# First 1x1 layer of a ConvNeXt block in fifteen products for eighteen, and the next image's first layernorm moved into fc1

## The chip, the core and the metric

The kernel runs on one core of a Trainium2 chip. The metric is the device time of one execution in microseconds (us). One execution was also recorded by the hardware profiler; the profile's stretches and timelines are counted from the start of that execution's span.

## What is computed

Eight images of 384 channels and 32 x 32 pixels go through two layers, all in fp32. Layer 0 is a transformer block, layer 1 a ConvNeXt block:

```python
# layer 0, on tokens (1024 per image, 384 wide), 8 heads of 48
xn  = layernorm(x);  q, k, v = xn @ w_qkv.T + b_qkv
x1  = softmax(q @ k.T * SCALE) @ v @ w_proj.T + b_proj + x
y   = x1 + gelu(layernorm(x1) @ w_fc1.T + b_fc1) @ w_fc2.T + b_fc2      # 384 -> 1536 -> 384
# layer 1
c   = depthwise_conv7x7(y) + dw_b
h   = gelu(layernorm(c) @ w1 + b1)                                      # 384 -> 1536
gx  = sqrt(sum over pixels of h**2);  nx = gx / (mean(gx) + eps)
out = y + (gamma * (h * nx) + beta + h) @ w2 + b2                       # 1536 -> 384
```

## The kernel before

Activations lie with channels on the 128 partitions and the 1024 pixels in the free dimension: three tiles of 128 channels (CT), twelve of the hidden width (HT), two halves of 512 pixels. A matrix product writes one PSUM bank of 128 x 512. TensorE (PE) does each such fp32 product in two passes, so the profile counts two matmuls for one in the source.

**Stages.** The loop over images interleaves two of them: after image b has gone through qk, attention, fc1 and fc2, the 1x1 layers w1 and w2 of image b-1 follow, with the values (v) of image b+1 between them. TensorE's order in the middle of the run is thus: qk(b), attention(b), fc1(b), fc2(b), w1(b-1), v(b+1), w2(b-1), qk(b+1). The last image is done apart, in pieces. VectorE (DVE) does the depthwise convolution of image b from w2(b-1) on, across the next image's attention; ScalarE (ACT) and accumulating DMAs from GpSimd (POOL) help it with seven taps per channel tile (`help_convolution`).

**Order of work.** The order is written out: nothing is rescheduled[...]. The class `Flow` keeps side work next to TensorE's: `flow.pe(us)` counts TensorE's time, and a chain (a generator) that yields a wait is continued when the count has come that far. `flow.finish(chain)` issues what is left of it. `after(first, chain)` starts a chain when another has ended.

**Fewer products.** fc2, w2 and qk multiply 3 x 3 by 3 x 2 blocks with fifteen products for eighteen. In fc2 and w2 (`by_thirds`) the hidden width is cut in three thirds of four tiles; the combinations of activations e, f, g, h, d are made in place between the fifteen products (four pairs of passes each, so 60 products), by DVE and, for `adding(g, f)`, `adding(h, b32)` and `adding(g, b32)`, by accumulating DMAs of 512 KB from POOL (`hid<-hid`, `y<-y`). In qk (`tiles_by_thirds`) one product is a single 128 x 512 one; its ten combinations of the input are made ahead by ten DVE subtractions and additions, `thirds_of`. The combined weights (`FORMS`) are made once, while image 0 is in attention, and kept in DRAM.

w1 (`grn_up`) works on six pairs of tiles; each takes eleven products for twelve, on four differences of the input that `block_differences` puts into `attn`. A `Weights` ring of nine tiles loads from SyncE's (SP) queue in the order of a plan; `used` frees a tile and issues the next load.

**Layernorms.** Per image there are three: ln1 before qk and the values, ln2 before fc1, ln3 before w1. `abreast` runs both halves of one side by side. Channel sums are made by folding the 128 partitions to 64 with an accumulating DMA from POOL (`ln_a<-ln_a`, `ln_sq<-ln_sq`, `attn<-attn`), then multiplying by ones on TensorE: two half-array products for each of sum and variance of each half. DVE adds, subtracts the mean and scales; ACT squares and takes rstd as exp(-0.5 ln(var + eps)).

Where ln1 and ln3 stand is decided by `conv_norm` (called in fc1, when ln2's second half is spawned) and `next_norms` (called at the end of fc1):

```python
        def conv_norm(b, ln):
            ...
                state["norm3"] = flow.spawn(after(ln, after(state["help"], after(state["conv"], norm))))
        def next_norms(b):
            ...
                state["norm1"] = flow.spawn(after(state["norm3"], norm, 50 if b else 11))
        def next_values(b):
                flow.finish(state["norm1"])
                state["thirds"] = flow.spawn(qk_thirds(b, state["xn"]))
                values(b, state["xn"])
```

So ln3 of image b-1 runs at the start of fc2(b), and ln1 of image b+1 in w1(b-1); for image 0, ln1 of image 1 runs in fc2(0). The tile `xn` has one buffer: it holds the normalized input of ln1, then that of ln2.

Of the kernel before, what the change touches and what calls it, by code (L numbers as in the profile page):

```python
# [51 lines left out]
P = 128  # L52
# [123 lines left out]
def block_kernel(  # L176
# [10 lines left out]
    w1: bass.AP,  # L187
    w2: bass.AP,
# [20 lines left out]
    s_w1 = dram.tile([P, HT // 2, 4, P], F32, tag="s_w1", bufs=1, name="s_w1")  # L209
# [7 lines left out]
    def load_x(b, tag, parts=2, engine=nc.sync):  # L217
        xt = one.tile([P, CT, N], F32, tag=tag, name=f"{tag}_{b}")
        src = image_of(x, b).rearrange("(c p) n -> p c n", p=P)
        for i in range(parts):  # L220
            cols = slice(i * N // parts, (i + 1) * N // parts)
            engine.dma_start(out=xt[:, :, cols], in_=src[:, :, cols])
        return xt

    vec = const.tile([P, NVEC], F32, name="vec")
    wqkv = const.tile([P, 3 * CT * C], F32, name="wqkv")
    wqk_sb = wqkv[:, : 2 * CT * C].rearrange("p (c m o) -> p c m o", c=CT, o=P)
    wv_sb = wqkv[:, 2 * CT * C :].rearrange("p (c o) -> p c o", c=CT)
    wproj_sb = const.tile([P, CT, C], F32, name="wproj_sb")
    ident = const.tile([P, P], F32, name="ident")  # L230
# [9 lines left out]
    third_e = const.tile([P, NH], F32, name="third_e")  # L240
# [112 lines left out]
    def plan_w1(tag, fast=True):  # L353
        plan = []
        for i in range(NC):
            plan.append(((f"w1_{tag}", i, "A"), chunk(w1, i)))
            if fast:
                plan.append(((f"w1_{tag}", i, "S"), s_w1[:, i, :, :].rearrange("p j o -> p (j o)")))
        return plan
# [28 lines left out]
    def thirds_of(src, places, e):  # L388

        b11, b12, b21, b22, b31, b32 = (src[:, s, half(n)] for s in range(CT) for n in range(2))  # L390
        f, h, e2, g, f2, h2, g2, f3, d = places
# [12 lines left out]
        return steps, (b12, b21, e, b22, f, h, e2, g, b31, f2, h2, g2, f3, b32, d)  # L404

# [138 lines left out]
    def weight_places(name):  # L544

        tiles = [three.tile([P, 2, NH], F32, tag="p", name=f"{name}_{i}") for i in range(2)]
        return [t[:, j, :] for t in tiles for j in range(2)]

# [30 lines left out]

    def qk(b, xn, weights=None):  # L580
# [3 lines left out]
        big = one.tile([P, HT * N], F32, tag="big", name=f"qk_{b}")  # L584
        parts = big[:, : 2 * NP * N].rearrange("p (i m n) -> p i m n", i=2, m=NP)
        if b == 0:
            spare_sums.append(big[:, 2 * NP * N :])
# [148 lines left out]
    def attention(b, xt, qT, kT, last_tile, ready, first):  # L736
# [44 lines left out]
        for n in range(len(steps) + 2):  # L781
# [10 lines left out]
            if n - 2 == len(steps) // 2 + 6:  # L792
                for chain in first:
                    flow.finish(chain)
                xn = one.tile([P, CT, N], F32, tag="xn", name=f"xn2_{b}")
# [20 lines left out]
    def exact_attention(xt, qT, kT):  # L816

        nc.vector.memset(attn, 0.0)
        for qt in range(N // P):
# [295 lines left out]
    def block_differences(acc):  # L1115

        b11, b12, b21, b22 = (acc[:, s, half(n)] for s in range(2) for n in range(2))
        t1, t2, t3, t4 = (attn[:, i, :] for i in range(4))
        yield 3.0
        for dst, one_, other in ((t1, b12, b11), (t2, b22, t1), (t3, b22, b12), (t4, b21, t2)):  # L1120
            nc.vector.tensor_tensor(dst, one_, other, ALU.subtract)
            yield 1.2

    def grn_up(b, acc, weights, tag):
# [5 lines left out]
        b11, b12, b21, b22, b31, b32 = (acc[:, s, half(n)] for s in range(CT) for n in range(2))  # L1130
        t1, t2, t3, t4 = (attn[:, i, :] for i in range(4))
        wa = f"w1_{tag}"
        spent = {}

        def finish(m):
            other_table(y[:, m, :], y[:, m, :], AF.Gelu, bias=b1[:, m : m + 1])

        def squares(i):
            for m in (i, i + HT // 2):
                waste = spent[i].rearrange("p a n -> p (a n)")  # L1140
                nc.scalar.activation(waste, y[:, m, :], AF.Square, accum_out=gx[:, m : m + 1])

        for i in range(HT // 2):
            j = i + HT // 2
            raw, sums = weights.at(wa, i, "A"), weights.at(wa, i, "S")
            a11, a12, a13, a22, a23 = (raw[:, k, :] for k in range(5))
            s1, s2, s3, s4 = (sums[:, k, :] for k in range(4))
            spent[i] = ps_s.tile([P, 2, NH], F32, tag="s", name=f"h_{b}_{i}_5")
            p5 = spent[i][:, 0, :]
            c11, c12, c21, c22 = (y[:, m, half(n)] for m in (i, j) for n in range(2))  # L1150

            def product(*pairs):
                bank = o_tile(f"h_{b}_{i}")
                accumulate(bank, list(pairs))
                return bank

            def plus(dst, bank, part):
                nc.vector.tensor_tensor(dst, bank, part, ALU.add)  # L1158

            nc.scalar.copy(c21, product((a11, b11)))  # L1160
            if i:
                finish(j - 1)
                squares(i - 1)
            plus(c11, product((a13, b31), (a12, b21)), c21)
            accumulate(p5, [(s1, t1)])
            plus(c21, product((s2, t2)), c21)
            plus(c12, p5, c21)
            plus(c12, product((s4, b22), (a13, b32)), c12)
            finish(i)
            plus(c21, product((s3, t3)), c21)  # L1170
            plus(c22, p5, c21)
            plus(c21, product((a23, b31), (a22, t4)), c21)
# [791 lines left out]
```

## Time and profile before

| | |
|---|---|
| time, median of 3 runs | 3287.62 us (3286.76 to 3288.6) |
| profiled execution: its time, its span | 3286.43 us, 3284.5 us |
| mean granted TensorE clock | 0.996 |
| busy: PE, DVE, ACT, POOL | 3262.0, 2413.3, 1630.0, 481.8 us |
| products `h` (w1), 792 passes in images 0 to 5 | 66 products an image |
| DVE additions of w1, `y<-h,y` | 288, 198.1 us, mean 690 ns |

A stage's length is read from the start of its first matmul to the start of the next stage's first. Ends of matmuls are modelled and overlap the next one, so a stage's lost time is its length less its passes, not less its busy time. In a timeline a line has the start, the duration, the engine, the source line, the operation, what it writes and reads, and in brackets how long the engine had been idle and what ended that.

### The profile page before, as it was taken

How to read it: one execution, taken by the hardware profiler on the slowest of the kernel's cores; microseconds unless marked ns; L12 is line 12 of the kernel's file. 1: busy time of each engine (PE TensorE's matmuls, PEld its weight loads, DVE VectorE, ACT ScalarE, POOL GpSimd, SP SyncE). 2: the span in 40 equal slices, each digit the busy share in tenths (PEclk: the TensorE clock that was granted, in tenths of full speed). 3: DMA queues.
4: the chain of work that ended last, by engine and by line, in shares of the span. 5: the costliest groups of instructions: out<-in, count | busy, mean ns of one | idle time of the engine just before them, and what ended most of it. 6: DMA issues, size and time to landing. Idle time of an engine off the chain costs nothing. (4 is left out here: it accounts for less than half of the span.)

```text
span 3284.5 us, 38862 instructions
## 1 busy us (share of the span) xinstructions
PE 3262.0 (99%) x14288; PEld 1410.0 (43%) x14288; DVE 2413.3 (73%) x3220; ACT 1630.0 (50%) x2243; POOL 481.8 (15%) x567
## 2 busy tenths in 40 slices
PE   9999999999999999999999999999999999999999
PEld 5334444443344434444334443444434444444455
DVE  4444787787867878678786787867887788879850
ACT  3542763447634375353762646526474365723631
POOL 2111210112110121101211012110221112200000
PEclk9999999999999999999999999999999999999999
DMA  6336733647345563536536374273843637433231
GB/s 236 115 109 146 166 61 78 154 111 171 60 97 144 135 139 58 127 116 169 102 61 140 106 188 82 56 169 87 202 74 61 179 88 189 74 79 85 68 91 54
DMA packets 202160, 380.08 MB, mean 116 GB/s; under 512 B 41072, under 2 KB 47088, under 8 KB 201328
## 3 DMA queue, kind: packets, MB, share of 16 engines
q0 software_dynamic: 80928, 161.78, 26.7%
q1 hardware_dynamic: 120752, 215.09, 21.3%
q8 instruction: 114, 1.87, 0.2%
q10 hardware_dynamic: 288, 0.71, 0.1%
q14 instruction: 78, 0.64, 0.1%
HBM read 197.25 MB, written 35.78 MB: 71 GB/s over the span
## 5 line engine op out<-in xcount | busy, mean ns | idle before, releaser
L1087 DVE SCALAR_TENSOR_TENSOR acc<-pad,vec,acc 128x870 f32<-128x870 f32 (+8 forms) x861 | 963.1, 1154 | 7.0 <-DMA acc<-tap 1.7
L756 ACT ACTIVATE p<-s 128x1024 f32<-128x1024 f32 x512 | 524.4, 1024 | 267.0 <-PE s L747 260.2
L747 PE MATMUL s<-qk 48*64 48x512 f32 x4096 | 537.9, 592 | 0.7 <-ACT qk L593 0.7
L767 PE MATMUL o<-p,v 64*64 64x512 f32 x4096 | 534.5, 589 | 0.0
L384 PE MATMUL fc<-xn,fc 128*128 128x512 f32 x1152 | 502.6, 595 | 2.0 <-DVE acc L509 2.0
L1109 POOL DMA_DIRECT2D acc<-tap x294 | 253.4, 868 | 1184.5 <-ACT tap L1108 698.6
L384 PEld LDWEIGHTS fc<-xn,fc 128*128 128x128 f32 x1152 | 218.6, 190 | 282.0 <-issue 271.6
L444 PE MATMUL fc_p<-hid,fc 128*128 128x512 f32 x728 | 319.3, 594 | 0.0
L456 ACT ACTIVATE hid<-fc,bfc_f 128x512 f32<-128x512 f32 x192 | 131.4, 686 | 339.8 <-PE fc L384 339.7
L767 PEld LDWEIGHTS o<-p,v 64*64 64x64 f32 x4096 | 162.2, 133 | 278.7 <-issue 272.8
L747 PEld LDWEIGHTS s<-qk 48*64 48x64 f32 x4096 | 158.4, 133 | 278.1 <-issue 225.9
L444 PE MATMUL o_p<-y,w 128*128 128x512 f32 x624 | 270.9, 592 | 0.0
L1158 DVE TENSOR_TENSOR y<-h,y 128x512 f32<-128x512 f32 x288 | 198.1, 690 | 93.6 <-PE h L444 80.4
L1108 ACT ACTIVATE tap<-pad,vec 128x512 f32<-128x512 f32 x294 | 215.9, 735 | 1.4 <-DMA acc<-tap 1.2
L444 PEld LDWEIGHTS fc_p<-hid,fc 128*128 128x128 f32 x728 | 137.4, 190 | 178.7 <-issue 174.9
L444 PE MATMUL h<-acc,w_A 128*128 128x512 f32 x432 | 207.4, 596 | 0.0
L444 PEld LDWEIGHTS o_p<-y,w 128*128 128x128 f32 x624 | 118.0, 190 | 148.7 <-issue 134.9
L1087 DVE SCALAR_TENSOR_TENSOR wqkv<-pad,vec,wqkv 128x377 f32<-128x377 f32 (+24 forms) x288 | 177.3, 686 | 0.6
L876 ACT COPY pad<-x 128x512 f32<-128x512 f32 x48 | 30.2, 635 | 253.6 <-DVE x L942 196.6
L708 DVE TENSOR_TENSOR attn<-o,attn 128x512 f32<-128x512 f32 x64 | 44.1, 689 | 152.1 <-ACT attn L706 152.1
L689 PE MATMUL proj<-attn,wproj_sb 128*128 128x512 f32 x288 | 127.3, 595 | 1.1 <-DVE attn L734 1.1
L444 PEld LDWEIGHTS h<-acc,w_A 128*128 128x128 f32 x432 | 80.6, 190 | 109.0 <-issue 93.4
(361 smaller groups left out, 3822.8 us busy)
## 6 DMA issues: line engine op xcount, KB each, us to landing
acc<-tap POOLq DMA_DIRECT2D x294, 256.0 KB, 3.6
w_A<-in_w SPq DMA_DIRECT2D x72, 384.0 KB, 3.3
fc<-s_fc SPq DMA_DIRECT2D x91, 256.0 KB, 4.3
hid<-hid POOLq DMA_DIRECT2D x42, 512.0 KB, 7.9
fc<-in_wfc SPq DMA_DIRECT2D x54, 384.0 KB, 4.2
w<-s_w SPq DMA_DIRECT2D x78, 256.0 KB, 2.6
y<-y POOLq DMA_DIRECT2D x36, 512.0 KB, 7.1
qk<-s_qk SPq DMA_DIRECT2D x42, 320.0 KB, 5.0
```

What stands on the lines that cost most here:

```text
L384: nc.tensor.matmul(out=ps, lhsT=lhsT(k), rhs=rhs(k)[:, half(h)], start=(k == 0), stop=(k == nk - 1))
L444: nc.tensor.matmul(out=bank, lhsT=lhsT, rhs=rhs, start=k == 0, stop=k == len(pairs) - 1)
L456: nc.scalar.activation(dst, src, function, **kw)
L689: nc.tensor.matmul(out=ps, lhsT=wproj_sb[:, m, ct * P : (ct + 1) * P], rhs=attn[:, m, :], start=(m == 0), stop=(m == CT - 1),)
L708: nc.vector.tensor_tensor(attn[:, m, :], outs[1], attn[:, m, :], ALU.add)
L747: nc.tensor.matmul(out=s[64 * i : 64 * i + 64, j, :], lhsT=kT[64 * j : 64 * j + HD, m, k0 : k0 + 64], rhs=qT[64 * j : 64 * j + HD, m, half ...
L756: nc.scalar.activation(p, s, AF.Exp)
L767: nc.tensor.matmul(out=outs[i][64 * j : 64 * j + 64, :], lhsT=v[keys, t, at : at + 64], rhs=p[keys, j, :], start=(t == 0), stop=(t == KT - 1),
L1087: nc.vector.scalar_tensor_tensor(dst, window, tap, dst, ALU.mult, ALU.add)
L1108: nc.scalar.mul(t.rearrange("p (h w) -> p h w", w=W), window, tap)
L1109: nc.gpsimd.dma_start(out=acc[:, ct, half(h)], in_=t, accum_op=ALU.add)
L1158: nc.vector.tensor_tensor(dst, bank, part, ALU.add)
```

## The change

Six parts, all visible in the diff:

1. w1 of images 0 to 5 is computed by `tiles_by_thirds`, in four groups of three tiles, from ten combinations of the layernorm's output (`make_thirds`) and fifteen combined weights per group; sums of products are copied by ACT or added by DVE as in qk.
2. Its combined weights are made from a new input layout `w1t`, group by group, by `sums_for_tiles` in image 0, along with those of qk. `w1_sums` in `prepare` goes.
3. The tile `xn` gets a second buffer; the room comes from wqk, which now lies in the large tile during image 0, from `ident` and from `third_e`. The next image is loaded in the middle of attention (`next_image`), not at the end of fc1.
4. ln1 of the next image is spawned in fc1, behind ln2's second half and ahead of ln3 of the previous image; ln3 now waits for it.
5. The combinations for qk are spawned after the values, and the first of them is made in place.
6. The last image's convolution writes into an `xn` buffer instead of the room of wqkv.

```diff
-        xt = one.tile([P, CT, N], F32, tag=tag, name=f"{tag}_{b}")
+        xt = one.tile([P, CT, N], F32, tag=tag, bufs=2 if tag == "xn" else 1, name=f"{tag}_{b}")
...
-    def thirds_of(src, places, e):
+    def thirds_of(src, name):
         b11, b12, b21, b22, b31, b32 = (src[:, s, half(n)] for s in range(CT) for n in range(2))
-        f, h, e2, g, f2, h2, g2, f3, d = places
+        f, h, e2, g = averages()
+        f2, d = (one.tile([P, NH], F32, tag=tag, name=f"{name}_{tag}") for tag in ("ln_a", "ln_rstd"))
+        h2, g2, f3 = (three.tile([P, NH], F32, tag="ln_sq", name=f"{name}_{i}") for i in range(3))
+        e = b11
         steps = (
             (e, b11, b12, ALU.subtract),
...
+    def make_thirds(what, src, name, us):
+        steps, thirds[what] = thirds_of(src, name)
+        for step in steps:
+            nc.vector.tensor_tensor(*step)
+            yield us
...
                 xn = one.tile([P, CT, N], F32, tag="xn", bufs=2, name=f"xn2_{b}")
+                next_image(b)
...
-    def block_differences(acc):
...
+        waste = ps_s.tile([P, N], F32, tag="s", name=f"h_{b}_squares")
+
+        def gelu(g, r):
+            m = g + 4 * (r - 1)
             other_table(y[:, m, :], y[:, m, :], AF.Gelu, bias=b1[:, m : m + 1])
...
+        def square(g, r):
+            m = g + 4 * (r - 1)
+            nc.scalar.activation(waste, y[:, m, :], AF.Square, accum_out=gx[:, m : m + 1])
+
+        for g in range(HT // CT):
+            tiles = {}
+
+            def bank(name):
+                name = "x" if name in "jqm" else name
+                if name not in tiles:
+                    tiles[name] = o_tile(f"h_{b}_{g}_{name}")
+                return tiles[name]
+
+            def behind(n):
+                if g and n == 3:
+                    gelu(g - 1, 2)
+                    gelu(g - 1, 1)
+                elif g and n == 1:
+                    square(g - 1, 2)
+                elif g and n == 4:
+                    square(g - 1, 1)
+                elif n == 14:
+                    gelu(g, 3)
+                elif n == 7:
+                    square(g, 3)
+
+            c = {f"c{r + 1}{n + 1}": y[:, g + 4 * r, half(n)] for r in range(CT) for n in range(2)}
+            for _ in tiles_by_thirds(weights, f"w1_{tag}", g, thirds["w1"], c, bank, behind):
+                pass
+        for what in (gelu, square):
+            for r in (2, 1):
+                what(g, r)
         return y, gx
...
         def conv_norm(b, ln):
 
+            if b + 1 < B:
+                xn = state["xn"]
+                norm = abreast(xn, xn, eps0, "g1", f"ln1_{b + 1}", True, gentle=True)
+                ln = state["norm1"] = flow.spawn(after(ln, norm))
             if b > 0:
                 acc = state["acc"]
                 how = dict(wait=5.0) if b < B - 1 else dict(wait=3.4, factor=2.4)
                 norm = abreast(acc, acc, eps1, "lnw", f"ln3_{b - 1}", True, **how)
                 if b < B - 1:
-                    norm = sequence(norm, block_differences(acc))
+                    norm = sequence(norm, make_thirds("w1", acc, f"w1_third_{b}", 1.4))
                 state["norm3"] = flow.spawn(after(ln, after(state["help"], after(state["conv"], norm))))
...
+        def next_image(b):
+            if b + 1 < B:
+                state["xn"] = load_x(b + 1, "xn")
+
+        def sums_for_tiles(i):
+            width = len(FORMS) * P
+            spare = large[0][:, (2 * NP + 2 * i) * N : (2 * NP + 2 * i + 2) * N]
+            for w, store, g in ((wqkt, s_qk, i), (w1t, s_w1, i), (w1t, s_w1, i + 2)):
+                yield from sums_singly(w[:, g * width : (g + 1) * width], store[:, g : g + 1], spare)
+                yield 8.0
...
-            if b + 1 < B:
-                xn = state["xn"] = load_x(b + 1, "xn")
-                name = f"ln1_{b + 1}"
-                places = (lambda: weight_places(name)) if b else averages
-                norm = abreast(xn, xn, eps0, "g1", name, True, places=places, gentle=b > 0, factor=1.4 if b else 1.7)
-                state["norm1"] = flow.spawn(after(state["norm3"], norm, 50 if b else 11))
...
                 flow.finish(state["norm1"])
-                state["thirds"] = flow.spawn(qk_thirds(b, state["xn"]))
                 values(b, state["xn"])
+                state["thirds"] = flow.spawn(make_thirds("qk", state["xn"], f"qk_third_{b}", 3.0))
...
-                singly = flow.spawn(after(None, sums_of_qk(), 1))
+                singly = [flow.spawn(after(None, sums_for_tiles(i), 33 + 5 * i)) for i in range(2)]
```

In `sums_singly` the waits of 14.0, 1.0 and 2.0 become 9.0, 0.6 and 1.0.

## The prediction

> **What bounds the kernel now.** I read the page's busy shares first, then stretches cut at the stages of one image, then the timelines of VectorE (DVE) and GpSimd (POOL) inside the stages that the change touches.
>
> ```profile
> span 3284.5 us, 38862 instructions
> ...
> PE 3262.0 (99%) x14288; PEld 1410.0 (43%) x14288; DVE 2413.3 (73%) x3220; ACT 1630.0 (50%) x2243; POOL 481.8 (15%) x567
> ```
>
> TensorE is busy 99% of the span, so every product removed counts in full, and so does every new wait of TensorE. An fp32 product is two passes: w2 has 60 products in 120 passes and takes 51.53 us below, so 0.4295 us a pass and 0.859 us a product. The stretches (length, then busy times of PE, PEld, DVE, ACT, POOL, the clock, the DMA share and GB/s) are fc2 of image 4, w1 of image 3, the values of image 5, w2 of image 3:
>
> ```profile
> core 0: us, PE busy (x) PEld busy (x) DVE busy (x) ACT busy (x) POOL busy (x), PEclk, DMA share, GB/s
> 1757.64:1811.57 53.93, 53.93 (x137) 23.05 (x136) 43.84 (x60) 12.50 (x20) 8.85 (x9) 1.00 0.73 176
> 1811.57:1870.85 59.28, 59.28 (x150) 25.24 (x149) 43.35 (x66) 37.17 (x52) 3.32 (x4) 1.00 0.39 120
> 1870.85:1886.55 15.70, 15.70 (x51) 9.34 (x50) 12.09 (x20) 12.66 (x20) 2.54 (x3) 1.00 0.25 51
> 1886.55:1938.08 51.53, 51.53 (x121) 22.71 (x120) 49.66 (x58) 12.07 (x14) 7.14 (x6) 1.00 0.66 153
> ```
>
> A layernorm adds 16 half-array passes to a stage, 2.06 us. Against the pure passes fc2 loses 0.3 us (53.93 - 51.54 - 2.06), w1 0.5 (59.28 - 56.69 - 2.06), w2 nothing. But DVE is busy 49.66 us of w2's 51.53: the cover there is nearly used up. POOL in fc2 of image 4:
>
> ```profile
> 1769.50 0.81 POOL L474 DMA_DIRECT2D ln_sq<-ln_sq  x1 [22.26 <-DVE ln_sq L523]
> 1770.89 0.80 POOL L474 DMA_DIRECT2D attn<-attn  x1 [0.59 <-DVE attn L523]
> ...
> 1779.66 1.19 POOL L954 DMA_DIRECT2D hid<-hid  x1 [5.16 <-ACT ln_rstd L534]
> 1781.37 1.21 POOL L954 DMA_DIRECT2D hid<-hid  x1 [0.53 <-PE fc_p L444]
> 1786.29 1.20 POOL L954 DMA_DIRECT2D hid<-hid  x1 [3.70 <-PE fc_p L444]
> 1788.01 1.19 POOL L954 DMA_DIRECT2D hid<-hid  x1 [0.52 <-PE fc_p L444]
> ```
>
> The third layernorm's variance folds leave early (12 us into fc2), and the last two adds, g += b32, leave as soon as product 8 has read g. DVE in w2 (start, duration):
>
> ```profile
> 1925.23 1.21 DVE L942 TENSOR_TENSOR y<-y 128x1024 f32<-128x1024 f32 x1
> 1926.37 1.18 DVE L1087 SCALAR_TENSOR_TENSOR acc<-pad,vec,acc 128x930 f32<-128x930 f32 x1
> 1927.46 1.22 DVE L942 TENSOR_TENSOR y<-y 128x1024 f32<-128x1024 f32 x1
> ...
> 1940.28 1.28 DVE L942 TENSOR_TENSOR kept<-o_p,kept 128x512 f32<-128x512 f32 x2
> ```
>
> The two y lines make f for product 13, which starts at 1886.55 + 12 x 3.436 = 1927.8: f is 1.3 us early, its second half 0.8. The last line reads the bank that the fifth product of qk writes next.
>
> [...] between 1888.3 and 1940 DVE runs its list without a gap. [...] the rows here show 0.68 to 0.69, starting 0.60 apart, or 0.72 where the next reads the last. [...] here the hid adds land after 5.2 to 10.1 (median 7.9 on the page)[...].
>
> **The change, part by part.**
>
> 1. w1: 66 products become 60 in each of images 0 to 5: 6 x 6 x 0.859 = **-30.9 us**. Combinations go from 48 DVE and 6 ACT to 44 and 20. Per group of 12.9 us, ACT has five copies (0.55), three gelus (1.06) and three squares (1.2), 9.5 us, and DVE eleven ops, 7.5 us. Walking the fifteen bank by bank, each write finds its bank read at least 0.3 us before, if a group starts on time: no cost. qk already runs such groups: 24.33 us for 56 passes (24.05). The tail up to the square root of gx ends some 6 us after w1; its matmul comes 7.7 us after, as now. Loads for w1 are twelve per image before and after, 3.84 MB, through the same ring on SP.
>
> 2. The next image's first layernorm (20 DVE ops, 6 squares, 4 Ln/Exp, two table loads, 4 folds on POOL, 16 passes) leaves w1 (image 1's leaves fc2 of image 0) and goes into the second half of fc1. The passes cost the same in either place. DVE is busy 29.8 of 54.06 us there, so 14 us more fit; the folds have 4 us to spare. Cost 0, from -0.5 to +1; image 1, where the convolution still runs, up to +2. xn is loaded some 120 us earlier (at the first projection instead of the end of fc1), on SP, into the second buffer: hidden (0 to +0.3 an image, behind small attention loads).
>
> 3. The third layernorm waits for the first, so its sums move from the start of fc2 to product 6 and its variance to product 11. **This is the costly part.** Times from the start of fc2, images 2 to 6: product 7 ends at 25.1. DVE then has the block that now runs from 1784.38 to 1791.23 (6.85 us), then four adds of squares (2.8): squares are ready at 33.5 and 34.9. Folds land 3.3 us (median) and 2.8 us after issue: 37.1 and 38.0. TensorE wants them at 36.25: 1.3 us lost. In the changed program's order, POOL has g += b32 *behind* these folds: it leaves at 35.9 and 37.6 instead of 27.3 and 29.0 and lands 6.3 and 8.1 later, at 42.1 and 45.7. Product 12 multiplies g and would start at 41.2: 0.9 and then 1.8 us more. fc2 ends **4.0 us late** (57.7 for 53.6); bounds 1.3 and 5.
>
> 4. Ten differences instead of four. DVE waits for g as well (f = f - g): its list from 45.7 is f and d (2.3), three adds of product 11 (1.8), d (1.1), six scalings (4.0), three differences (1.9), six adds of product 13 (3.8), then the fourth difference at 61.3 and the ninth at 66.3. w1 wants the fourth for its second product at 58.6 (2.8 us lost), the ninth for its fifth (2.4), and the third product's bank read (0.4): **5.6 us**; bounds 1.0 and 7.2.
>
> 5. The differences for qk start after the values, not among them. Before, five stand in the values stage, where DVE has 3.6 us idle. After, four of them (2.4 us) come where w2's DVE list has no gap: f is 1.1 and 0.5 us late for product 13, and qk's fifth product finds its bank 0.9 us late: **2.5 us**; bounds 0 and 3.
>
> 6. Preparation: six small sums (18 ops each on 128 columns) instead of one of 256 columns and w1's four. DVE is busy 35 to 44% of attention in image 0: hidden, 0 to +2 (second layernorm's fold behind 1.5 MB of loads on POOL). Image 0's fc2 takes 58.98 us for 53.6, 1.9 of it waiting for the first layernorm's fold and the rest near half clock (PEclk 0.97); without it -5.4. Sum **-3.5** (-5.4 to +2).
>
> Image 1 has all six adds ahead of the folds, so g is not held: 1.0 + 1.7 + 2.5 = 5.2 us lost, where fc2, w1 and qk lose 2.7 + 0.8 + 0.3 = 3.8 now. Images 2 to 6: 4.0 + 5.6 + 2.5 = 12.1 for 1.1 now, so +11.0 each. Sum: -30.9 - 3.5 + 1.4 + 5 x 11.0 = **+22 us**. The profiled execution took 3286.4 (span 3284.5 and 1.9 around it): 3308.4, and 1.2 more for the median of 3287.62: **3310**.
>
> **The rivals.**
>
> A, forecast: 3310 (own range 3296 to 3322). B: g lands in time, by shorter landings or an issue that isn't held; then 1.3 + 1.7 + 2.5 = 5.5 in each of images 2 to 6, net 4.4: -30.9 - 3.5 + 1.4 + 22 = -11, **3277**. For it: DMA times scatter from 5.2 to 10.1. Against: POOL's order puts the folds first, and their input needs product 7's block. C, the other side: the cover holds as it does now, waits as before: -30.9 - 3.5 = **3253**. For it: w2 hides 49.66 us of DVE work and loses nothing. It decides if the ninth difference is there 3.4 us after w1 starts. Against: DVE has 13 us of ops behind product 11. D: the gaps of w1 reach 2.4 and 2.8 us; in image 0 a gap of 1.9 us was followed by some 1.7 us of passes at half rate. One such penalty an image (images 2 to 6) and 1.5 more of late banks: +16, **3326**. That the fifteen aren't fifteen is excluded: the program's order shows sixty w1 products an image.
>
> **How the numbers follow.** Chances: A 0.54, D 0.16, B 0.22, C 0.08. 0.2% (6.6 us) is about what a measurement can tell from no change. Faster: C 0.08 and 0.14 of B; same: 0.08 of B and 0.04 of A; slower: 0.50 of A and D. So 0.22, 0.12, 0.66. The range takes A and D and B but its fastest end: 3266 to 3332.
>
> **What would show it.** Right: fc2 of images 2 to 6 near 57.7 us with TensorE waiting for a variance fold and then for hid from a DMA; w1 near 57 us (51.5 without loss), its gaps released by DVE's attn and third tiles; w2 above 53. Wrong in step 3: g lands before 41 us of fc2. Wrong in 4: w1 below 53. If w1's gaps come from ACT or from banks inside later groups, step 1 is wrong. If fc1 grows by more than 3 us, step 2 is.

## The result, and the profile after

| | before | after |
|---|---|---|
| median | 3288.11 us (3286.76 to 3291.29, 4 runs) | 3336.93 us (3336.07 to 3339.06, 4 runs) |
| ratio, 95% interval | | 1.0148 (1.013 to 1.0166) |
| profiled execution | 3286.43 us | 3337.68 us |

The change costs 48.8 us (51.4 between the two profiled spans); 22 were forecast, with a range that ended 5 us below the measurement. The direction was right, the size was not. The page of the changed kernel:

```profile
span 3335.9 us, 38888 instructions
...
PE 3263.2 (98%) x14216; PEld 1406.6 (42%) x14216; DVE 2429.6 (73%) x3318; ACT 1677.6 (50%) x2329; POOL 480.8 (14%) x567
```

There are 72 fewer passes of TensorE in the records, and TensorE is busy 1.2 us longer all the same: passes got slower. The span grew by 51.4 us. Cut at the start of each image's values, it splits like this (image 0: from the span's start to the values of image 1). "Images 2 to 6" below means these stretches; the w1 and w2 inside one belong to the image before it.

| | forecast | measured |
|---|---|---|
| image 0 | -3.5 | 327.58 to 336.28: +8.7 |
| image 1 | -3.75 | -0.25 |
| images 2 to 6 together | +29.3 | +9.3, +10.5, +5.7, +8.0, +8.4: +41.9 |
| last image | 0 | +1.0 |

So 12.2 us of the miss are in image 0, 12.6 in images 2 to 6 (2.5 each), 3.5 in image 1, 1.0 in the last. The stretches of one image, columns as in the prediction: fc2 of image 3, w1 of image 2, values of image 4, w2 of image 2.

```profile
core 0: us, PE busy (x) PEld busy (x) DVE busy (x) ACT busy (x) POOL busy (x), PEclk, DMA share, GB/s
1382.53:1441.69 59.16, 56.76 (x137) 23.86 (x136) 42.36 (x57) 11.54 (x19) 10.51 (x10) 0.97 0.63 138
1441.69:1500.77 59.08, 53.74 (x122) 23.23 (x121) 37.20 (x58) 36.97 (x56) 0.00 (x0) 0.97 0.34 111
1500.77:1516.47 15.70, 15.70 (x51) 9.34 (x50) 9.92 (x16) 13.68 (x22) 2.55 (x3) 1.00 0.25 50
1516.47:1569.75 53.28, 52.07 (x122) 22.54 (x120) 51.42 (x61) 12.07 (x14) 7.13 (x6) 1.00 0.64 148
```

PEclk is what to see first: 0.97 in fc2 and w1, where it was 1.00. w1 has 120 passes for 132 and no layernorm, which should be 51.5 us; it takes 59.1, as long as before. w2 is 1.75 us longer with the same products. A wait is given below as the time lost from start to start, against a full-speed pass; the bracket in a timeline, which ends at the modelled end of the pass before, is some 0.16 us less. TensorE late in fc2, and POOL ahead of it:

```profile
1419.51 1.08 PE L483 MATMUL ln_var<-ln_sq,ones 64*64 64x512 f32 x4 [0.41 <-DMA ln_sq<-ln_sq]
1422.58 1.08 PE L483 MATMUL ln_var<-attn,ones 64*64 64x512 f32 x4 [1.99 <-DMA attn<-attn]
1423.59 18.27 PE L447 MATMUL fc_p<-hid,fc 128*128 128x512 f32 x38
```

```profile
1416.68 0.85 POOL L477 DMA_DIRECT2D ln_sq<-ln_sq  x1 [10.44 <-DVE ln_sq L526]
1418.07 0.80 POOL L477 DMA_DIRECT2D attn<-attn  x1 [0.54 <-DVE attn L526]
1418.61 2.71 POOL L967 DMA_DIRECT2D hid<-hid  x2
```

The two adds of g stand behind the folds, as forecast. The second fold is issued 35.5 us into fc2 (forecast 35.2) and used at 40.05, so it took 4.5 us where 2.8 were allowed; that makes 1.7 of the 2.7 us that TensorE waits for the two folds. The four passes of fc2 behind it take 0.81 to 0.86 us from start to start instead of 0.43 (from 1423.59 on), at a granted clock of 0.53 (1423.60 to 1427.00). TensorE at the start of that w1:

```profile
1441.69 1.02 PE L418 MATMUL h_n<-attn,w 128*128 128x512 f32 x2
1445.17 1.13 PE L418 MATMUL h_k<-w_third,w 128*128 128x512 f32 x2 [2.46 <-DVE w_third L406]
1446.14 1.02 PE L418 MATMUL h_x<-acc,w 128*128 128x512 f32 x2
1450.04 1.12 PE L418 MATMUL h_n<-attn,w 128*128 128x512 f32 x2 [2.88 <-ACT y L439]
1451.00 1.78 PE L418 MATMUL h_z<-w_third,w 128*128 128x512 f32 x2
1452.57 1.91 PE L418 MATMUL h_x<-acc,w 128*128 128x512 f32 x2
```

There are two waits, before the second and the fourth product; then two products that take 1.8 to 1.9 us instead of 1.0: these are passes at half rate, 0.72 to 0.86 us from start to start instead of 0.43, and the granted clock between 1451.0 and 1454.3 is 0.52. The second wait is released by ACT's copy of the first product's bank, and ACT's timeline says why it is late:

```profile
1443.89 0.63 ACT L889 COPY pad<-x 128x512 f32<-128x512 f32 x1 [9.17 <-DVE x L955]
1446.35 0.63 ACT L889 COPY pad<-x 128x512 f32<-128x512 f32 x1 [1.83 <-DVE x L955]
1448.28 1.24 ACT L889 COPY pad<-x 128x512 f32<-128x512 f32 x2 [1.29 <-DVE x L955]
1449.42 0.57 ACT L439 COPY y<-h_n 128x512 f32<-128x512 f32 x1
```

The copy of `h_n` stands behind four copies of fc2's output into `pad`, and these wait for fc2's last adds on DVE, which stand among the ten differences. DVE itself:

```profile
1425.04 1.23 DVE L955 TENSOR_TENSOR hid<-hid 128x1024 f32<-128x1024 f32 x1 [5.41 <-DMA hid<-hid]
1429.41 2.36 DVE L955 TENSOR_TENSOR hid<-hid 128x1024 f32<-128x1024 f32 x2 [3.15 <-DMA hid<-hid]
...
1444.43 0.68 DVE L406 TENSOR_TENSOR w_third<-attn,acc 128x512 f32<-128x512 f32 x1
...
1449.48 0.69 DVE L406 TENSOR_TENSOR w_third<-w_third_ln_a,w_third 128x512 f32<-128x512 f32 x1
```

From fc2's start at 1382.53 the two halves of g are there after 42.5 and 46.9 us (forecast 42.1 and 45.7), the fourth difference after 62.6 (61.3) and the ninth after 67.6 (66.3). The DVE and POOL lists of the forecast were right to 1.3 us. What TensorE paid for them was not. In w2 and qk of the same image it was:

```profile
1558.83 1.98 PE L447 MATMUL o_p<-y,w 128*128 128x512 f32 x4 [0.96 <-DVE y L955]
1561.06 8.85 PE L447 MATMUL o_p<-y,w 128*128 128x512 f32 x20 [0.25 <-DVE y L955]
1573.94 1.13 PE L418 MATMUL qk_z<-qk_third,qk 128*128 128x512 f32 x2 [0.60 <-DMA fc<-in_wfc]
```

Product 13's two halves are 1.1 and 0.4 us late and qk's fifth product 0.8 (forecast 1.1, 0.5 and 0.9). The last bracket names a load, but DVE's add that reads the bank ends at 1573.89, just before the product.

### The profile page after: what moved, and what is told of

The parts are those of the page before. It is cut to its first block, busy times and chain, and to the rows that moved or that the text cites. A ratio compares the mean times of both kernels' runs of the same rounds, so it can differ in the third digit from the quotient of the medians.

```text
span 3335.9 us, 38888 instructions
## 1 busy us (share of the span) xinstructions
PE 3263.2 (98%) x14216; PEld 1406.6 (42%) x14216; DVE 2429.6 (73%) x3318; ACT 1677.6 (50%) x2329; POOL 480.8 (14%) x567
## 5 line engine op out<-in xcount | busy, mean ns | idle before, releaser
L757 PE MATMUL s<-qk 48*64 48x512 f32 x4096 | 547.3, 593 | 0.7 <-ACT p L766 0.4
L777 PE MATMUL o<-p,v 64*64 64x512 f32 x4096 | 544.6, 591 | 0.0
L447 PE MATMUL fc_p<-hid,fc 128*128 128x512 f32 x728 | 328.3, 608 | 0.0
L777 PEld LDWEIGHTS o<-p,v 64*64 64x64 f32 x4096 | 166.4, 133 | 277.5 <-issue 269.2
L1100 DVE SCALAR_TENSOR_TENSOR acc_last<-pad,vec,acc_last 128x377 f32<-128x377 f32 (+24 forms) x288 | 177.3, 687 | 0.6
L540 DVE SCALAR_TENSOR_TENSOR xn<-xn,vec,ln_rstd 128x512 f32<-128x512 f32 x69 | 48.9, 747 | 112.8 <-ACT ln_rstd L537 112.8
L677 PE MATMUL v<-wv_sb,xn 128*128 128x384 f32 x384 | 126.8, 487 | 0.0
L434 DVE TENSOR_TENSOR y<-h_n,y 128x512 f32<-128x512 f32 x72 | 49.8, 692 | 76.3 <-PE h_n L418 74.0
```

The source lines that it names most:

```text
L447: nc.tensor.matmul(out=bank, lhsT=lhsT, rhs=rhs, start=k == 0, stop=k == len(pairs) - 1)
L677: nc.tensor.matmul(out=ps[:, :C], lhsT=xn[:, k, t * P : (t + 1) * P], rhs=wv_sb[:, k, :], start=(k == 0), stop=(k == CT - 1),)
L757: nc.tensor.matmul(out=s[64 * i : 64 * i + 64, j, :], lhsT=kT[64 * j : 64 * j + HD, m, k0 : k0 + 64], rhs=qT[64 * j : 64 * j + HD, m, half ...
L777: nc.tensor.matmul(out=outs[i][64 * j : 64 * j + 64, :], lhsT=v[keys, t, at : at + 64], rhs=p[keys, j, :], start=(t == 0), stop=(t == KT - 1),
L1100: nc.vector.scalar_tensor_tensor(dst, window, tap, dst, ALU.mult, ALU.add)
```

## The experiments

Each edit is against the changed kernel unless it says otherwise. The times are medians; they stand against 3336.93 for the changed kernel and 3287 to 3290 for the kernel before, measured again beside each group of runs. "Attention of image 0" leaves out the projection: 120.2 us in the kernel before, 132.5 in the changed one.

**e1: prepare() as late as before.** The change took w1's sums out of `prepare`, so everything behind them moved forward.

```diff
         weights.release()
+        yield 26.0
         yield from shift_through_w2()
```

> One line added to the changed kernel: a pause of 26 us of TensorE time in prepare(), where the four small sums of w1 stood before the change, so that the gbeta and w2 loads of image 0 are issued as late as they were. The six small sums stay. Changed kernel: 3336.9 us; its image 0 lost 8.7 us where 3.5 were forecast as a gain. Theory 1 (the six sums pulled prepare() forward: gbeta's work and the second layernorm's fold then stand in the same DVE list and POOL queue as the loads of w1t and w2; in the trace these are gaps of TensorE of 5.8 us at 121 and of 2.4 us at 174, with half-rate passes of 2.7 and 1.1 us behind them): both gaps go, image 0 shortens by 9 to 12 us, about 3326. Rival (the loads of w1t themselves delay DVE, wherever prepare() stands): a gap of like size appears elsewhere in attention of image 0, 3334 to 3338.

Measured: 3334.02 (ratio to before 1.0136). Both gaps named are gone, and attention of image 0 falls from 132.5 to 125.9 us. But gbeta's next column sum waits 2.4 us at 145.7, and fc1's second half grows by 1.9 us: image 0 gains 3.9, not 9 to 12. Theory 1 holds for half of the loss in attention (6.6 of 12.3 us); what makes the rest is taken up in e12.

**e2: a quicker first layernorm.**

```diff
-                norm = abreast(xn, xn, eps0, "g1", f"ln1_{b + 1}", True, gentle=True)
+                norm = abreast(xn, xn, eps0, "g1", f"ln1_{b + 1}", True)
```

> The first layernorm inside fc1 without its small pauses (gentle off): in flow time it takes some 26 us for 38, so the third layernorm behind it starts and folds some 12 us earlier. All else as in the changed kernel (3336.9 us; fc2 and w1 together 116.5 us in images 2 to 6, 113.0 in image 1). Theory 2 (time is lost because the third layernorm waits for the first, which makes the variance folds, and behind them the ten differences, late): fc2 and w1 together fall to 106 to 109 us in images 2 to 6, and the gaps before the variance folds and before h_k and h_n go: about 3290 to 3300. Rival 2 (the fifteen products lose time by themselves, in the banks, ACT or DVE of their groups): w1 stays near 57 us, under 10 us in all, 3327 or more. Rival 3 (DVE has no room in the second half of fc1 for a quicker layernorm): fc1 grows by 2 us or more an image, 3335 or more.

Measured: 3325.27. fc2 and w1 together, 114.9 to 118.2 us in the changed kernel, take 111.2 to 113.3 in images 2 to 6: half of the fall that was expected. The gap at the variance folds is gone. In its place the six scalings and four of the differences now stand ahead of f's first half in DVE's list, and product 13 waits 2.43 us for it, 46.6 us into fc2 (here of image 3):

```profile
1426.20 1.21 DVE L955 TENSOR_TENSOR hid<-hid 128x1024 f32<-128x1024 f32 x1
```

```profile
1427.51 6.66 PE L447 MATMUL fc_p<-hid,fc 128*128 128x512 f32 x11 [2.26 <-issue]
```

w1 is 52.57 us in three of the five images, with a single wait of 0.96: the fifteen products lose next to nothing inside their groups, so rival 2 falls. fc1 grows by 1.7 to 1.9 us (rival 3, in part).

**e3: the qk differences earlier.**

```diff
-                values(b, state["xn"])
-                state["thirds"] = flow.spawn(make_thirds("qk", state["xn"], f"qk_third_{b}", 3.0))
+                values(b, state["xn"], range(KT // 2))
+                state["thirds"] = flow.spawn(make_thirds("qk", state["xn"], f"qk_third_{b}", 1.6))
+                values(b, state["xn"], range(KT // 2, KT))
```

> The ten differences for qk start behind the fourth of eight value tiles, 1.6 us apart, instead of behind the eighth and 3.0 apart. All else as in the changed kernel (3336.9 us; w2 53.28 and qk 24.99 us in every image, 51.53 and 24.33 before). Theory 3 (the differences are late in DVE's full list of w2): most are made in the values stage, where DVE is busy 63%; w2 falls to 51.5 to 52, qk to 24.3 to 24.6: 1.5 to 2.4 us in each of six images, 3322 to 3328. Rival (w2 loses its time to something else, for instance the convolution's start or y's scalings): w2 stays at 53, 3335 to 3338.

Measured: 3320.89, 16 us less. w2 is 51.53 us in every image, exactly as before the change: 6 x 1.75 = 10.5 us shown. qk did not fall as expected: it takes 24.1 to 25.7 us, 24.9 on average as in the changed kernel. The other 5 to 6 us are scattered (w1 lost 5.2 us less over six images, fc2 2.1 more) and not assigned.

**e4: w1 of before.** `grn_up`, `block_differences`, `plan_w1` and w1's four sums in `prepare` are those of the kernel before.

> The changed kernel with w1 of before: eleven products for six tiles, four differences, w1's four small sums in prepare() and two sums for qk alone. The first layernorm inside fc1, the second buffer and the late qk differences stay. By my sums (the moved layernorm costs fc2 4 us and a half-rate stretch of 1.6 us in images 2 to 6, w2 and qk 2.4 in all): image 0 back to 316 to 320 us, w1 57.2 and four differences that wait little, fc2 near 58: 3315 to 3325. If the fifteen products themselves lost time inside their groups, w1 and fc2 would come out at 111 us together and the whole at 3290 to 3305. If the moved layernorm cost nothing and everything were lost to the ten differences: fc2 54, w1 57, 3290 to 3300 as well, told apart by fc2's own length.

Measured: 3329.34, 4 us above the expected range. Stretches fc2 of image 3 and w1 of image 2:

```profile
1371.51:1430.24 58.73, 56.76 (x137) 23.86 (x136) 42.31 (x57) 11.55 (x19) 10.51 (x10) 0.97 0.63 139
1430.24:1487.94 57.70, 56.92 (x133) 25.00 (x132) 37.41 (x56) 30.34 (x42) 0.00 (x0) 1.00 0.34 114
```

With w1 undone, fc2 is as long as with it (58.73 and 59.16; 58.9 and 59.5 on average over images 2 to 6): the loss in fc2 comes from the moved layernorm. w1 is 57.7 and its clock 1.00: TensorE loses about 1 us where the ten differences cost it over 5. Attention of image 0 is 119.0 us: its loss comes from the new way of making w1's sums, which is their operations, their transfers and the place of `prepare` together.

**e5: the fifteen products alone.** ln1 goes back into w1 (`next_norms` of before), with places and totals of its own, since w1's banks take all four tiles of `ps_o`:

```diff
+        own = one.tile([P, CT, N], F32, tag="xn", bufs=2, name=f"ln1_own_{b}").rearrange("p c n -> p (c n)")
...
+                totals.append(ps_s.tile([P, N], F32, tag="s", name=f"ln1_totals_{b}"))
...
+                norm = abreast(xn, xn, eps0, "g1", name, True, each=each, gentle=b > 0, factor=1.4 if b else 1.7)
+                state["norm1"] = flow.spawn(after(state["norm3"], norm, 56 if b else 11))
```

> The fifteen products alone: the first layernorm of images 2 to 7 goes back inside w1 (that of image 1 into fc2 of image 0), with buffers of its own (the second xn buffer, two p tiles and one PSUM tile for its totals), and x is loaded at the end of fc1 as before. The late qk differences and the six small sums stay as in the changed kernel (3336.9 us). Theory 2 (the fifteen are good for their 5.15 us an image, and what is lost in fc2 and w1 comes from the third layernorm having to wait for the first): fc2 54 to 55, w1 53.6 (51.54 and 2.06 of layernorm) to 55, fc1 53.2, so each of images 1 to 6 is some 2 us shorter than before the change, with the 2.4 us of w2 and qk still lost; image 0 keeps its loss in attention and pays fc2's 59 us again: about 3285 to 3297. Rival (ten differences and a layernorm in w1 are too much for DVE, so w1 is late wherever the layernorm stands): w1 57 or more, 3310 or more.

Measured: 3313.01, above what was expected. Stretches fc2 of image 3 and w1 of image 2, then ACT late in that w1:

```profile
1383.19:1437.12 53.93, 53.93 (x137) 23.05 (x136) 45.34 (x62) 12.39 (x20) 8.80 (x8) 1.00 0.72 175
1437.12:1495.26 58.14, 56.37 (x138) 22.47 (x136) 41.36 (x65) 43.49 (x66) 3.34 (x4) 1.00 0.40 122
```

```profile
1479.74 1.28 ACT L455 ACT_TABLE_LOAD   x1
1481.04 0.69 ACT L536 ACTIVATE ln_own<-ln_totals,eps 128x512 f32<-128x512 f32 x1
...
1483.53 0.57 ACT L439 COPY y<-h_n 128x512 f32<-128x512 f32 x1
```

fc2 with all ten differences in it is back at 53.93 us without a wait: ln3's start decides, not the number of differences. But w1 takes 58.1 for a nominal 53.6. The rival had the length right; that DVE is full is not what the trace shows, since it is busy 41 us of 58. Of the 4.5 us lost, 1.65 are two waits for ACT's copies out of w1's banks (the second behind the table load and the logarithms of ln1 above), about 0.9 are waits for DVE's additions, and 0.6 are the layernorm's own sums, beyond their 2.06; the rest are delays of 0.1 us each. No run separates these. With ln1 inside w1 the fifteen products bring 1.1 of their 5.15 us (58.1 for 59.28).

**e6: a first combination.** e5 with the edits of e1, e3 and e7, and ln1 of image 1 in fc1.

> e5 with the qk differences behind the fourth value tile (e3), prepare() late (e1), 20 us instead of 9 between a load of the small sums and its first use, and the first layernorm of image 1 inside fc1 of image 0. By the parts: images 1 to 6 as in e5 less 2.3 us each in w2 and qk, so some 4 us shorter each than before the change; image 0 near 314 us as before the change (attention 120 to 122, fc1 56 to 60, fc2 51.5): 3258 to 3268 us, faster than both kernels. If DVE is too full in w1: 3290 or more. If the qk differences behind the fourth value tile collide with the layernorm that now ends in w1: the values and w2 stages grow by 1 us or more an image, 3268 to 3275.

Measured: 3301.67. w1 stays at 57.5 to 58.5 us as in e5, and image 0 takes 331.6 from the values on (314.5 before). The 20 us cost time by themselves, as e7 shows; how much of the 17 us is theirs is not shown.

**e7: more time between the small sums' loads and their use.**

```diff
-        yield 9.0
+        yield 20.0
```

> The changed kernel with one number changed: 20 us instead of 9 of TensorE time between each load of the six small sums and its first VectorE use. Theory 1a (VectorE, working its list in order, stands before loads of w1t that take 10 us to land, and gbeta's work stands behind it): the gap of 5.8 us at 121 us goes, with its half-rate passes, 8 us: about 3329; the gap at 174 us stays. Rival (the gbeta loads themselves are late behind other transfers): the gap stays, 3335 to 3338.

Measured: 3343.96, slower. The gap at 121 us goes, and one of 4.6 us comes at 106.5 before a column sum of `w_lnb`, another of 2.6 in the projection. So the gap that theory 1a named does go, but two others come, and the run doesn't tell what makes them. e12 leaves out the operations that wait for w1's loads.

**e8: TensorE kept busy in the waits.** The three products do none of the reference's work.

```diff
+                if isinstance(b, int) and b and g == 0 and slot in (1, 4):
+                    for _ in range(3):
+                        nc.tensor.matmul(out=waste[:, :NH], lhsT=ones, rhs=thirds["w1"][0], start=True, stop=True)
```

> The changed kernel with three idle products (ones times a block of acc, 2.58 us, into a PSUM tile that is not in use yet, results dropped) ahead of the second and of the fifth product of w1's first group in images 2 to 6, where TensorE waited 2.6 and 3.0 us. They do no work of the reference. Theory [...]: the waits are filled, the half-rate passes behind them go, and though no difference comes earlier w1 gets 1.3 to 1.6 us shorter in images 2 to 6: about 3329. If the half rate has another cause, w1 stays (58 to 59 us with both fillers) and the time is 3336 to 3340; if the waits are shorter than the fillers in several images, longer still.

Measured: 3342.41, not shorter. TensorE in w1 of image 3:

```profile
1849.05 2.74 PE L1172 MATMUL h_squares<-acc,ones 128*128 128x512 f32 x6
1851.63 1.02 PE L420 MATMUL h_k<-w_third,w 128*128 128x512 f32 x2
1852.48 1.02 PE L420 MATMUL h_x<-acc,w 128*128 128x512 f32 x2
1855.12 1.13 PE L420 MATMUL h_n<-attn,w 128*128 128x512 f32 x2 [1.61 <-ACT y L441]
1856.08 2.74 PE L1172 MATMUL h_squares<-acc,ones 128*128 128x512 f32 x6
1858.65 1.02 PE L420 MATMUL h_z<-w_third,w 128*128 128x512 f32 x2
```

The first wait is filled, and no product behind it is slow (0.86 us from start to start): in w1 of images 2 to 6 no half-rate passes are left (1.55 to 1.76 us of them in four of five without fillers), while image 0's w1, which has no fillers, loses 1.8 us to them behind a wait of 2.2. So in w1 it is the idling that brings the half rate. The time did not fall because the second wait stood before the fourth product, on ACT; the second filler, before the fifth, only added 2.6 us.

**e9: the late pad copies behind w1's first copies.** The last four of fc2's six copies into `pad` are put on a list (`later`) and issued in w1's first group, when `behind` is called with n = 12; `load_kept` moves behind `grn_up`.

```diff
+            later.append(lambda: pad_half(xt, r, n))
...
+                if g == 0 and n == 12:
+                    while later:
+                        later.pop(0)()
```

> The changed kernel (3336.9 us) with the last four copies of fc2's output into pad put behind the copies that ACT makes for w1's first group, in images 1 to 6 (and the reload of kept put behind w1 with them). In the changed kernel's trace TensorE waits 3.0 us before the fourth product of w1 for ACT's copy of the first product's bank, and ACT stands before the pad copies, which wait for fc2's last adds on DVE, behind the ten differences. Theory: that wait goes; the fifth product then waits for the ninth difference, by the DVE list some 2.3 us; so w1 shortens by 0.5 to 1 us in images 2 to 6, by 2 us in image 1: 3328 to 3335. Rival (the fourth product waits for DVE too, ACT is only the last named): w1 unchanged, 3336 to 3338. If the reload of kept comes too late for w2: w2 grows, above 3340.

Measured: 3332.28. TensorE in w1 of image 2:

```profile
1444.25 1.02 PE L418 MATMUL h_x<-acc,w 128*128 128x512 f32 x2
1445.11 1.02 PE L418 MATMUL h_n<-attn,w 128*128 128x512 f32 x2
1448.34 2.01 PE L418 MATMUL h_z<-w_third,w 128*128 128x512 f32 x2 [2.21 <-DVE w_third L406]
```

The fourth product no longer waits; the fifth does, for the ninth difference. So two waits end here close together, and taking ACT's away leaves DVE's: 2.4 us for 3.0. It also shows that on ACT the waiting copies held the one behind them: with the four moved, the fourth product, which needs the copy of `h_n`, starts 0.86 us after the third (1444.25, 1445.11) and not 3.90 (1446.14, 1450.04 in the changed kernel).

**e10: a second combination.** e1, e3, e9, and

```diff
-                norm = abreast(xn, xn, eps0, "g1", f"ln1_{b + 1}", True, gentle=True)
+                norm = abreast(xn, xn, eps0, "g1", f"ln1_{b + 1}", True, wait=4.4 if b else 3.4, gentle=b < 2)
...
-                    norm = sequence(norm, make_thirds("w1", acc, f"w1_third_{b}", 1.4))
+                    norm = sequence(norm, after(None, make_thirds("w1", acc, f"w1_third_{b}", 1.0), 5.0))
```

> The changed kernel with five edits: the first layernorm in fc1 without pauses but with longer waits for its folds (images 3 to 7), the ten differences 5 us later and 1.0 us apart, the qk differences behind the fourth value tile, the late pad copies of e9, prepare() late as in e1. By e1, e2, e3 and e9: image 0 318; w2 and qk as before the change; fc1's second half 56 to 58.5, fc2 53 to 54.5, w1 51.6 to 53, where before the change fc1, fc2 and w1 took 166.4 together: 161 to 166. So images 2 to 6 0 to 5 us shorter each than before, image 1 some 4 us: 3265 to 3292, likeliest 3277, faster than before by 0.3%. If DVE has no room for it (differences still late, or fc2's own f late): 168 to 170 and 3300 or more.

Measured: **3271.53**, ratio to the kernel before **0.9948 (0.9934 to 0.9962)**: 17 us faster than before, 65 faster than the changed kernel. fc1's second half and fc2 of image 3, w1 and w2 of image 2:

```profile
1304.85:1361.50 56.65, 56.08 (x141) 23.89 (x140) 42.46 (x54) 30.24 (x43) 9.97 (x11) 1.00 0.34 67
1361.50:1415.43 53.93, 53.93 (x137) 23.05 (x136) 41.88 (x57) 11.61 (x18) 8.90 (x8) 1.00 0.67 149
1415.43:1468.12 52.69, 52.03 (x121) 22.61 (x120) 32.87 (x51) 36.94 (x56) 0.00 (x0) 1.00 0.31 95
1483.83:1535.36 51.53, 51.53 (x122) 22.71 (x121) 50.53 (x60) 12.07 (x14) 7.13 (x6) 1.00 0.66 153
```

fc1, fc2 and w1 take 163.3 us for 166.4 before, at full clock. The fifteen products bring nearly what step 1 said once nothing is late: w1 52.7 for 57.2 (59.28 less the layernorm's 2.06), 4.5 of 5.15 us. Alone, the edits of e1, e2, e3 and e9 gave 2.9, 11.7, 16.0 and 4.7 us, 35 together; the other 30 come with their combination, the longer waits for the folds and the later start of the ten differences, which were not run apart. Nor were these edits tried on the kernel before.

**e11: e10 with the small sums in one chain of 256 columns.**

> e10 with the six small sums of 128 columns in two chains made into three of 256 columns in one chain, 14 us between load and first use; so VectorE has 54 operations of about 0.35 us for 108 of 0.22 in image 0, and 1.97 MB in one load for two of 0.98. Theory 1 (image 0's loss is VectorE's and POOL's crowded list in attention): attention of image 0 120 to 123 us for 125.9 in e1, and 3 to 6 us less than e10 in all. Rival (it is the transfers, 11.8 MB in and out, whatever their grouping): attention of image 0 as in e1 or longer, e10 or slower.

Measured: 3292.58. Not conclusive: a gap of 16.2 us came ahead of the last qk tile of image 0, which waits for the load of 1.97 MB. Attention of image 0 took 126.3 us for e10's 124.2, so the grouping is no help there.

**e12: the small operations left out.**

```diff
+        if not made:
+            yield 5.8
+            nc.gpsimd.dma_start(out=store, in_=t)
+            return
...
-                yield from sums_singly(w[:, g * width : (g + 1) * width], store[:, g : g + 1], spare)
+                yield from sums_singly(w[:, g * width : (g + 1) * width], store[:, g : g + 1], spare, w is wqkt)
```

> The changed kernel with the 72 small VectorE operations of w1's four sums left out (its four loads of 0.98 MB and four stores stay, so w1 multiplies by zeros where sums should be; the qk sums stay). It leaves out that part of the computation. Open since e7 and e11: whether image 0's 12 us in attention come from VectorE's crowded list or from the transfers and POOL's queue. If VectorE's list: attention of image 0 falls from 132.5 to 120 to 123 us, 3324 to 3328. If the transfers and the queue: the gap before gbeta's column sum at 121 us, or one like it, stays, attention 129 to 133, 3333 to 3338. The gap at 174 us (the second layernorm's fold behind six w2 loads on POOL) should stay in either case.

Measured: 3337.12, attention of image 0 136.6 us. Without the 72 operations the gap before gbeta's column sum is longer, 7.9 us for 5.8. DVE in the changed kernel, then in e12:

```profile
110.00 0.49 DVE L1374 TENSOR_TENSOR qk<-qk 128x128 f32<-128x128 f32 x2 [5.97 <-DMA qk<-in_w1t]
...
114.95 0.20 DVE L725 RECIPROCAL inv<-sums 128x8 f32<-128x8 f32 x1 [4.06 <-DMA sums<-attn]
115.08 1.50 DVE L1374 TENSOR_TENSOR qk<-qk 128x128 f32<-128x128 f32 x6
116.49 1.82 DVE L1510 TENSOR_TENSOR w_gbeta<-w_gbeta,vec 128x768 f32<-128x768 f32 x2
```

```profile
100.53 0.68 DVE L718 TENSOR_TENSOR attn<-o,attn 128x512 f32<-128x512 f32 x1
115.52 0.20 DVE L725 RECIPROCAL inv<-sums 128x8 f32<-128x8 f32 x1 [14.31 <-DMA sums<-attn]
115.72 1.83 DVE L1514 TENSOR_TENSOR w_gbeta<-w_gbeta,vec 128x768 f32<-128x768 f32 x2
```

DVE stands 14.3 us before attention's own 4 KB transfer of softmax sums. It is under way beside 4.9 MB of loads and stores from POOL's queue, which take 71% of the DMA engines' time between 100 and 118 us. gbeta's scaling stands behind that reciprocal (115.72 after 115.52), its column sum behind the scaling (120.32), and attention's next products behind the column sum (120.80).

So the small operations are not the cause. The late transfer alone is not either: from its issue on SP to the reciprocal it took 10.9 us in the changed kernel, but also 10.9 in e4 and 8.6 in the kernel before, where no work of TensorE stood behind it. What is new is the order: taking w1's sums out of `prepare` put gbeta's scaling behind that reciprocal, and e1, which puts it back, regains 6.6 of 12.3 us. For the other half the transfers are what is left (30.5 MB between 57 and 215 us, 21.8 before; 7.9 and 3.1 of them for w1's sums), by exclusion: no run leaves out w1's loads and stores alone.

**e13: e10 with the quick layernorm in image 1 too** (`gentle=b < 1`).

> e10 (3271.5 us) with the first layernorm without pauses in image 1's fc1 too. There e10 takes 54.8 + 61.1 + 54.5 = 170.4 us for fc1's second half, fc2 and w1, because the third layernorm is still late; e2 took 58.5 + 53.9 + 55.1 = 167.5 with it quick. Theory: image 1 gets 3 to 5 us shorter, nothing else moves: 3266 to 3269. Rival (the convolution that still runs in image 1's fc1 leaves DVE no room): fc1 grows by what fc2 gains, 3270 to 3274.

Measured: 3271.28, ratio 0.9953 (0.994 to 0.9967), no different from e10. The rival was right: in image 1, fc2 falls from 61.1 to 53.9 and w1 from 54.5 to 52.7, and fc1 grows from 54.8 to 62.3, where the convolution still fills DVE (busy 89%).

## Why the prediction was wrong

1. *w1: -30.9, no cost inside the groups.* Right: e2 (three images) and e10 have w1 at 52.6 to 52.7, what is left beyond 51.5 being one wait at its start. A gap of w1 released by ACT was named as a sign against this step. It came, but in the first group and from fc2's copies, which e9 moves, so it falls to step 4.

2. *ln1 in fc1 at no cost.* Nearly: fc1's second half is 2.7 us longer in images 2 to 6, 2.06 of it the moved passes, 0.6 not foreseen.

3. *fc2 4.0 us late; 1.3 for the folds, 2.7 for g behind them.* The place is right (e4: fc2 58.7 with the layernorm alone), the size is not: 59.5 on average, 5.9 over its nominal 53.6. TensorE waited 2.7 us for the variance folds, not 1.3, because the second fold took 4.5 us to land and 2.8 were allowed (both of image 3; in images 2 to 6 the wait ends 39.9 to 40.4 us into fc2). With the slow passes behind that wait, g came 0.3 us ahead of its product (second half there after 46.9, wanted after 47.15): the wait for hid that the step forecast did not occur. About 2 us more an image are **half-rate passes**, which the forecast's sum left out; they stood in the prediction as rival D with a chance of 0.16, although the records of before had shown them behind a gap of 1.9 us. The last 1.2 are small delays between passes and are not assigned.

4. *w1 5.6 us late.* 5.5 measured on average (2.3 to 7.5), but by another composition, so the agreement is luck: about 4 of waits and 1.3 of half-rate passes. The second wait was put at the fifth product, for the ninth difference. It came at the fourth, on ACT: the step asked what stands behind DVE's wait on DVE, and not what ACT holds behind DVE's late adds. e9 shows the wait that was forecast, once ACT's is gone. (That a waiting operation holds what stands behind it on its engine was the author's assumption; e9 shows it for ACT's copies, e12 for DVE, where gbeta's scaling starts 0.20 us after the reciprocal that stood for 14.3.)

5. *w2 and qk 2.5.* Right, in size and place: w2 +1.75 and qk +0.66, with the waits where they were forecast, and e3 takes w2's away.

6. *Image 0: -3.5; sums hidden in idle DVE time.* **This step failed most**, 12.2 us. It priced the sums by DVE's idle share, and asked neither what moves forward in `prepare` when w1's sums leave it nor what their bytes do to other transfers. e4 shows that the new way of making w1's sums is the cause, e12 that their operations on DVE are not, e1 that the earlier `prepare` makes half of it: it puts gbeta's scaling behind a late 4 KB transfer (5.8 us of TensorE's time at 121), and the second layernorm's fold behind six w2 loads in POOL's queue (2.4 us at 174), where the step allowed 2 for the whole. What makes the rest stays open; 8.7 MB more on the DMA engines are its likeliest source. The second term of the step was right: fc2 and fc1 of image 0 gave -7.5 + 2.5 = -5.0 for -5.4.

Image 1 has waits of 1.4 and 2.2 us and half-rate passes as the others, 3.5 more than the 5.2 allowed for. Of the rivals, B and C fall; D was the nearest, 3326: it had the half-rate passes, though at w1's gaps alone and not at fc2's, and nothing of image 0.

## What to carry to other kernels

Work that moves earlier may delay what was made to wait for it: here a layernorm with time to spare was put in front of one with none, and a gain of 31 us became a loss of 49; with the same parts and other starts it is a gain of 17. Follow a late operation through every engine's list, to the copies that free the banks, and ask of hidden preparation what it moves forward and what its bytes delay, as well as what its operations cost. Add to each new wait of TensorE the half-rate passes behind it: here 40 of the 61 lone waits of 1.75 to 3.25 us had them, mostly for 1.7 to 1.8 us, and 2 of the 196 of 0.75 to 1.25 us.

## What the runs showed of the hardware

**The clock.** Take the waits of TensorE that stand alone in the fifteen traces of this case (no other wait over 0.4 us within 5 us before or behind), and count those with more than 1.25 us lost in the 5.5 us behind them, which is three passes of 0.85 us instead of 0.43. Of 196 waits between 0.75 and 1.25 us, 2 were of this kind; of 26 between 1.25 and 1.75 us, 4; of 61 between 1.75 and 3.25 us, 40, mostly with four slow passes, 1.7 to 1.8 us; of 14 over 3.75 us, all, for up to 3.1 us. So waits of 1.75 to 3.25 us had slow passes behind them two times in three. The same wait (2.43 us in e2's fc2) is followed by four slow passes in three images and by none in two, so a single trace doesn't tell its price.

**DVE's additions.** The prediction's 0.68 to 0.69 us are fp32 additions and subtractions of 128x512 in the kernel before. They start 0.60 us apart (1793.09, 1793.69), or 0.72 where one reads what the last wrote (1788.57, 1789.29).

**Small transfers beside large ones.** The 4 KB transfer of softmax sums, from its issue on SP to the reciprocal that waits for it: 2.0 us at 88.4 us in the kernel before, with the DMA engines 4% busy; 8.6 at 103.3 in the same trace, 84% busy; 14.3 in e12, 94% busy with loads of about 1 MB from another queue.
